# Expert matmuls with gate and up columns in one operand, down products one pair later, rows in blocks of 128

## The chip, the core and the metric

The kernel runs on one core of a Trainium2 chip. The core has TensorE (PE: matmuls, with weight loads PEld beside them), VectorE (DVE), ScalarE (ACT), GpSimd (POOL) and SyncE (SP), and 16 DMA engines that all queues share. The metric is the device time of one execution in microseconds, as the median of several runs. Profiles are taken from one execution, and all times in them count from the start of its span.

## The reference

The kernel computes four layers of cross attention and feed-forward on x of 4 x 256 rows of 256, each added to x after a layer norm. The change lies in the last step alone, a mixture of 64 experts of which every row chooses 8:

```python
x = hidden_states.reshape(-1, h)                       # 1024 rows of 256
router_logits = x @ gate_w                             # 64 logits
routing_weights, selected = jax.lax.top_k(router_logits, K)   # K = 8
routing_weights = jax.nn.softmax(routing_weights, axis=-1)
...
gate = jax.lax.ragged_dot(hidden_sorted, gate_proj_w, group_sizes)   # 256 -> 96
up = jax.lax.ragged_dot(hidden_sorted, up_proj_w, group_sizes)       # 256 -> 96
down = jax.lax.ragged_dot(jax.nn.silu(gate) * up, down_proj_w, group_sizes)  # 96 -> 256
...
out = jnp.sum(out * routing_weights[..., None], axis=1)
```

Everything is float32 in this step.

## The kernel before

All layers ahead of the experts run in one planned stretch (`layers`), with TensorE, VectorE, ScalarE, GpSimd and SyncE in a written order. At its end each tile of 128 rows is normed, routed, and scattered row by row to a table `hs` in device memory: expert e owns rows 192 e to 192 e + 191 (`CAP = 192`). A row of `hs` has 257 words, 256 of data and one with the number of its place in the results. There are 64 scatters of 128 rows, 8 choices for each of 8 tiles, issued by GpSimd (L1674). Rows that no token claims hold a number out of range, and are skipped when results are written. The tables `hs` and `yd` are filled early on by SyncE from constant tiles, `hs` in rows of 1,028 bytes and `yd` in rows of 1,024.

The experts are worked off in 32 pairs. `fill_rows` loads the 384 rows of a pair into a tile `hb` of 128 partitions x 3 rows: in the kernel before, partition q holds rows 3q, 3q+1 and 3q+2, one run of 3,084 bytes, and the first 64 partitions belong to the first expert. The loads of the first four pairs go to memory of earlier stages and are issued in `layers` by `first_rows` (the tiles `q`, `q`, `q`, `wmask` in the profile); each waits for the scatters of the choices that can reach its experts. Later ones run `AHEAD` = 6 pairs ahead in six buffers.

Weights come in groups of four experts (`load_weights`: 768 KB of gate and up, 384 KB of down, two DMAs), six groups in buffers `wt`. Groups 0 and 1 are loaded inside `layers` into memory that has become free (`cx` and `ctxT`). Weights and rows all go through SyncE's queue in the order of the code.

One pair, in the order of the code (`experts`):

- TensorE: gate sums `ps_g` and up sums `ps_u` (L1925), for each of two experts and two halves of the 256 inputs a matmul with 96 columns of weights against 192 rows, 8 in all
- ACT: `g` = silu(gate) (L1931); DVE: `act` = up x g (L1933), both over 96 x 384
- TensorE: the next pair's rows are transposed in 6 blocks of 128 x 128 (`rows_turned`, L1851), and copied to `hbT`, one half by ACT (L1936) and one by DVE (L1937)
- TensorE: down sums `ps_y` (L1943), for each of 3 rows of a partition and each expert a matmul with 64 columns of `act` against the 256 columns of `dn`, to the lower or upper 64 partitions
- DVE copies two of the three results to `yb` and ACT one (L1948); GpSimd puts them with three indirect DMAs (L1950) to `yd`, by the place numbers in `hb`
- beside that: in pairs 0 to 7 DVE works out the choice weights of one tile each (L1842 to L1844); in pairs 8 to 31 it makes diagonal matrices `diag` (L1965); loads of rows and weights are issued; from pair 23 on results are loaded back from `yd` (`load_results`, L1873) and some are added to x by DVE (L1885)

After the last pair `sums` adds the remaining results, half of the tiles by matmuls with `diag` (L1890), and stores x.

TensorE, DVE, ACT, POOL and SP execute in the order of the code here. f32 matmuls show as two records each in the profile, transposes as one. A branch with `rwo` handles rows that exceed an expert's 192 places; it is jumped over in this run.

Of the kernel before, what the change touches and what calls it, by code (L numbers as in the profile page):

```python
# [23 lines left out]
I32 = mybir.dt.int32  # L24
# [32 lines left out]
CAP = 192  # L57
RPP = 2 * CAP // P
# [172 lines left out]
def model(ctx: ExitStack, tc: tile.TileContext, a: dict, out: bass.AP):  # L231
# [155 lines left out]
    def expert_parts(gu, dn):  # L387
        return (
            gu.rearrange("p (e c i) -> p e c i", e=GROUP, c=4), dn.rearrange("p (e d) -> p e d", e=GROUP)
        )  # L390
# [35 lines left out]
    def fill_rows(p, since):  # L426

        ld = nc.sync.dma_start(
            hbs[p].rearrange("p j d -> p (j d)"),
            hs[2 * p * CAP : 2 * (p + 1) * CAP, :].rearrange("(p j) d -> p (j d)", p=P),  # L430
        )
        wanted = [i for n, js in zip(since, puts[: 2 * p + 2]) for i in js[n:]]
        needs(ld, "put", wanted, "rows of these choices alone")

    def layers(nk):
# [892 lines left out]
        def first_rows():  # L1328
            for p in range(in_early):
                yield Op(SP, 0.06, PUT[2 * p : 2 * p + 2], kb=386)  # L1330
                fill_rows(p, before)
# [422 lines left out]

    wts = [moe_tile([P, GROUP * (4 * I3 + D)], "wt", WEIGHTS)]
# [10 lines left out]
    def load_rows(p):  # L1766
        hbs[p] = moe_tile([P, RPP, HW], "hb", AHEAD)
        fill_rows(p, [0] * K3)
# [29 lines left out]
    with tc.If(rv > 0):  # L1798
# [9 lines left out]
        with tc.For_i(0, E3, 1) as e:  # L1808
# [4 lines left out]
            for c in range(NCH):  # L1813
                pg, pu = ps_mm([I3, CH], "ps_g3"), ps_mm([I3, CH], "ps_u3")
                for k, ps in enumerate((pg, pu)):
                    for dc in range(2):
                        o = (2 * k + dc) * I3
                        nc.tensor.matmul(
                            ps, gu[:, o : o + I3], hTs[c][:, dc, :], start=dc == 0, stop=dc == 1
                        )  # L1820
                g = moe_tile([I3, CH], "g_left", 1)
                nc.scalar.activation(g, pg, AF.Silu)
                nc.vector.tensor_mul(g, pu, g)
                for k in range(TPC):
                    t = c * TPC + k
                    y = ps_acc([P, D], "ps_y")
                    nc.tensor.matmul(y, g[:, k * P : (k + 1) * P], dn, start=True, stop=True)
                    w = scal(1, "w_left")
                    nc.vector.tensor_copy(w, rwo[:, t, bass.ds(e, 1)])
                    nc.vector.scalar_tensor_tensor(x_t(t), y, w, x_t(t), ALU.mult, ALU.add)  # L1830

    silu = small.tile([P, 1], F32, tag="silu", name="silu", bufs=1)
    diag = moe_tile([P, NT // 2, len(ON_PE), P], "diag", 1)
# [12 lines left out]
    def rows_turned(p):  # L1846
        hb, hbT = hbs[p], moe_tile([P, 2, RPP, P], "hbT", 2)
        tps = [ps_tp([P, RPP, P], "tp_hb") for _ in range(2)]
        for dc, tp in enumerate(tps):
            for j in range(RPP):  # L1850
                nc.tensor.transpose(tp[:, j, :], hb[:, j, dc * P : (dc + 1) * P], ident)  # L1851
        return hbT, tps
# [53 lines left out]

    def experts():
        for p in range(in_early, AHEAD):
            load_rows(p)
        load_weights(FIRST)  # L1910
        load_weights(FIRST + 1)
# [3 lines left out]
        hbT, tps = rows_turned(0)  # L1915
        nc.scalar.copy(hbT[:, 0], tps[0])
        nc.vector.tensor_copy(hbT[:, 1], tps[1])
        for p in range(n_pairs):
            e = 2 * p
            gu, dn = weights[e // GROUP]  # L1920
            pg, pu = ps_mm([I3, 2, RPP, P // 2], "ps_g3"), ps_mm([I3, 2, RPP, P // 2], "ps_u3")
            for k, ps in enumerate((pg, pu)):
                for i in range(2):
                    for dc in range(2):
                        nc.tensor.matmul(  # L1925
                            ps[:, i], gu[:, (e + i) % GROUP, 2 * k + dc, :],
                            hbT[:, dc, :, i * (P // 2) : (i + 1) * (P // 2)],
                            start=dc == 0, stop=dc == 1,
                        )
            g = moe_tile([I3, 2, RPP, P // 2], "g4", 2)  # L1930
            nc.scalar.activation(g, pg, AF.Silu)  # L1931
            act = moe_tile([I3, 2, RPP, P // 2], "act3", 2)
            nc.vector.tensor_mul(act, pu, g)  # L1933
            if p + 1 < n_pairs:
                hbT, tps = rows_turned(p + 1)
                nc.scalar.copy(hbT[:, 0], tps[0])  # L1936
                nc.vector.tensor_copy(hbT[:, 1], tps[1])  # L1937
            yb = moe_tile([P, RPP, D], "yb", 3)
            for js in ((0, 1), (2,)):
                y = ps_acc([P, len(js), D], "ps_y")  # L1940
                for k, j in enumerate(js):
                    for i in range(2):
                        nc.tensor.matmul(  # L1943
                            y[i * (P // 2) : (i + 1) * (P // 2), k], act[:, i, j, :],
                            dn[:, (e + i) % GROUP, :], start=True, stop=True,
                        )
                for k, j in enumerate(js):
                    (nc.scalar.copy if j == 1 else nc.vector.tensor_copy)(yb[:, j, :], y[:, k, :])  # L1948
            for j in range(RPP):
                put = nc.gpsimd.indirect_dma_start(  # L1950
                    out=yd[:, :],
                    out_offset=bass.IndirectOffsetOnAxis(
                        ap=hbs[p][:, j, D : D + 1].bitcast(I32), axis=0
                    ),
                    in_=yb[:, j, :], in_offset=None, bounds_check=NPAIR - 1, oob_is_err=False,
                )
                tc.declare_no_dep(put.ins, group="back", reason="distinct rows")
                tc.add_to_no_dep_group("back", put.ins)
                backs.append(put.ins)

            if p < NT:
                choice_weights(p)
            n, m = len(on_pe), n_pairs - NT
            for t, j in on_pe[max(p - NT, 0) * n // m : max(p - NT + 1, 0) * n // m]:
                nc.vector.tensor_scalar(  # L1965
                    diag[:, t // 2, j - ON_PE[0], :], ident, choice_w[:, t, j : j + 1], None, ALU.mult
                )
            if p + AHEAD < n_pairs:
                load_rows(p + AHEAD)
            k = FIRST + 2 + p if p < WEIGHTS - 2 else p // 2 + WEIGHTS if p % 2 else 0  # L1970
            if k and k < E3 // GROUP:
                load_weights(k)
            if p in loaded:
                load_results(loaded[p], p)
            for t, j in added_at.get(p, ()):
                add_result(t, j)
# [48 lines left out]

def laid_out(i):
# [38 lines left out]
        "w3_gu": gu.reshape(2, E3, 2, P, I3).transpose(3, 1, 0, 2, 4).reshape(P, E3, 4, I3),  # L2065
# [20 lines left out]
```

## Time and profile before

| what | value |
|---|---|
| median of 6 runs | 684.26 us (682.97 to 689.56) |
| the profiled execution | 686.94 us, span 685.2 us |
| start of pair 0's gate sums | 492.66 us |
| start of pair 1's gate sums | 500.36 us |
| start of pair 31's gate sums | 657.37 us |
| last put issued | 665.32 us |
| PE busy in the span | 612.9 us (89%) |
| POOL busy in the span | 401.9 us (59%), of it 96 puts of 0.97 us or a little more |

The profile's page gives for each engine the busy time in the span, and groups of instructions with the mean time of one. The stage table gives the same by stretches of time, with the granted clock of TensorE (1.00 is full) and the share of time that the 16 DMA engines were busy. The timeline lists instructions in order of time: start, length, engine, line, operation, output<-inputs, shapes, count of merged records, and in brackets how long the engine had been idle and what ended that.

From 500 to 600 us the pairs follow each other at 4.99 to 5.00 us, with one of 5.55 at 540. From 596.6 to 602 ACT and DVE were for the most part idle without a cause that the profile names, and the pairs that began at 595.83 and 604.94 took 9.11 and 6.64 us. Pair 30, beginning at 651.50, took 5.87. The end, from pair 31's gate sums to the end of the span, takes 27.8 us.

### The profile page before, as it was taken

What the parts mean: (1) busy time and instruction counts of PE and PEld (TensorE: products, weight loads), DVE (VectorE), ACT (ScalarE), POOL (GpSimd) and SP (SyncE); (2) the same over time, 40 slices, a digit from 0 to 9 for tenths busy, and PEclk for the clock granted to TensorE, in tenths of its full rate; (3) what the DMA queues carried; (4) which work ended last, traced back from release to release, by engine and by line L of the source; (5) the groups of instructions that cost most, each with busy time, mean ns of one, the idle gap of its engine ahead of it and who ended that gap; (6) DMA issues with size and microseconds to landing.
All of it is one profiled execution on the core that took longest, in us unless ns stands there. A gap on an engine that the chain in (4) does not pass through costs nothing. (4 is left out here: it accounts for less than half of the span.)

```text
span 685.2 us, 11415 instructions
## 1 busy us (share of the span) xinstructions
PE 612.9 (89%) x3831; PEld 469.3 (68%) x3844; DVE 444.7 (65%) x1094; ACT 349.7 (51%) x899; POOL 401.9 (59%) x531
## 2 busy tenths in 40 slices
PE   5998799989999999999999899397399999989965
PEld 4763367676787778778687678265377778868754
DVE  5688757876968795799786556344377544333655
ACT  2143248879788763667875875384322222222210
POOL 7997985045464536558268587717745655635650
PEclk9998899999999999999999999789599999989997
DMA  9999999611100230000031110202579988766567
GB/s 304 369 374 198 199 199 234 186 25 47 62 2 1 62 108 2 0 1 1 2 116 39 62 63 30 95 9 77 166 238 305 308 294 277 246 202 197 172 207 250
DMA packets 57059, 98.15 MB, mean 143 GB/s; under 512 B 7121, under 2 KB 39624, under 8 KB 56992
## 3 DMA queue, kind: packets, MB, share of 16 engines
q1 hardware_dynamic: 47072, 78.40, 40.2%
q0 software_dynamic: 7680, 16.84, 7.2%
q10 hardware_dynamic: 2240, 2.10, 1.0%
q8 instruction: 32, 0.52, 0.3%
q14 instruction: 35, 0.29, 0.1%
HBM read 58.42 MB, written 43.07 MB: 148 GB/s over the span
## 5 line engine op out<-in xcount | busy, mean ns | idle before, releaser
L1950 POOL DMA_INDIRECT yd<-yb,hb x84 | 83.2, 991 | 63.7 <-DVE yb L1948 44.4
L1674 POOL DMA_INDIRECT hs<-hx,slots x64 | 65.5, 1023 | 26.7 <-issue 13.7
L881 POOL TENSOR_TENSOR st<-st,mhalf 128x1 f32<-128x1 f32 x56 | 32.9, 591 | 56.5 <-DVE st L877 44.2
L1933 DVE TENSOR_TENSOR act<-ps_u,g 96x384 f32<-96x384 f32 x32 | 17.7, 554 | 49.6 <-ACT g L1931 24.7
L1505 POOL TENSOR_TENSOR q<-rt 64x512 f32<-64x512 f32 x32 | 42.5, 1328 | 10.9 <-DVE rt L1501 7.6
L1943 PE MATMUL ps_y<-wt,act 96*64 96x256 f32 x336 | 43.7, 397 | 5.7 <-DVE act L1933 4.5
L1538 ACT ACTIVATE e<-ps_s,nm 128x128 f32<-128x128 f32 x128 | 45.6, 393 | 5.6 <-DVE nm L1532 4.8
L1925 PE MATMUL ps_g<-hbT,wt 128*96 128x192 f32 x224 | 44.5, 343 | 0.0
L1948 DVE COPY yb<-ps_y 128x256 f32<-128x256 f32 x64 | 25.3, 422 | 28.2 <-PE ps_y L1943 25.4
L1925 PEld LDWEIGHTS ps_g<-hbT,wt 128*96 128x96 f32 x224 | 35.0, 167 | 11.4 <-issue 11.1
L1925 PE MATMUL ps_u<-hbT,wt 128*96 128x192 f32 x224 | 41.3, 328 | 0.0
L1948 ACT COPY yb<-ps_y 128x256 f32<-128x256 f32 x32 | 11.9, 372 | 54.9 <-DVE yb L1948 37.5
L1925 PEld LDWEIGHTS ps_u<-hbT,wt 128*96 128x96 f32 x224 | 36.8, 165 | 0.1
L1943 PEld LDWEIGHTS ps_y<-wt,act 96*64 96x64 f32 x336 | 22.1, 139 | 20.9 <-DVE act L1933 9.6
L1526 PEld LDWEIGHTS ps_s<-keys,q 128*128 128x128 f32 x256 | 35.4, 200 | 1.4
L1526 PE MATMUL ps_s<-keys,q 128*128 128x128 f32 x256 | 35.5, 284 | 0.0
L1576 PE MATMUL ps_u<-e,kvc 128*64 128x512 f32 x64 | 22.9, 633 | 13.5 <-ACT e L1562 11.3
L1931 ACT ACTIVATE g<-ps_g 96x384 f32<-96x384 f32 x32 | 15.6, 486 | 38.0 <-PE ps_g L1925 18.0
L1450 POOL TENSOR_TENSOR hh<-g,v 128x512 f32<-128x512 f32 x16 | 20.2, 1275 | 23.8 <-ACT g L1448 20.0
L1936 ACT COPY hbT<-tp_hb 128x384 f32<-128x384 f32 x31 | 14.8, 478 | 34.0 <-PE tp_hb L1851 16.0
L1532 DVE TENSOR_REDUCE nm<-ps_s 128x4 f32<-128x512 f32 x32 | 21.5, 684 | 16.4 <-remote 11.3
L1259 ACT ACTIVATE qT<-tp_q,rnd 128x512 bf16<-128x512 f32 (+2 forms) x48 | 25.7, 567 | 10.8 <-PE tp_q L1255 10.7
(344 smaller groups left out, 1726.2 us busy)
## 6 DMA issues: line engine op xcount, KB each, us to landing
hs<-order SPq DMA_DIRECT2D x1, 12336.0 KB
hb<-hs SPq DMA_DIRECT2D x28, 385.5 KB
wt<-in_w_gu SPq DMA_DIRECT2D x14, 768.0 KB
yd<-order SPq DMA_DIRECT2D x1, 8192.0 KB
wt<-yd SPq DMA_DIRECT2D x6, 1024.0 KB
wt<-in_w_dn SPq DMA_DIRECT2D x14, 384.0 KB
wo<-in_w_o SPq DMA_DIRECT2D x2, 1024.0 KB
w<-in_w SPq DMA_DIRECT2D x2, 704.0 KB
```

Of the source, the lines that this page charges most:

```text
L881: nc.gpsimd.tensor_tensor(s[:, 8:9], s[:, 7:8], mhalf, ALU.pow)
L1259: nc.scalar.activation(qT[:, 4 * i : 4 * i + full, :], tp.ap[:, :full, :], AF.Identity, bias=rnd[:, 1:2])
L1505: nc.gpsimd.tensor_add(qv(q[i])[r, hps, :], t0[r], t1[r])
L1526: nc.tensor.matmul(s.ap[:, k, :], qv(q[hd % 2])[:, hd // 2, rows], keys3[:, hd % 2, b * S : b * S + nk * P], start=False, stop=k == n - 1,)
L1532: nc.vector.tensor_reduce(nm[:, :n], s.ap, AX.X, ALU.max, negate=True)
L1538: nc.scalar.activation(wide[:, k, :], s.ap[:, k, :], AF.Exp, bias=nm[:, k : k + 1], accum_out=tot[:, k : k + 1],)
L1576: nc.tensor.matmul(o[r], kvc[:, 2 * b + kc, :], e[:, :, kc, :], start=kc == 0, stop=kc == nk - 1)
L1674: put = nc.gpsimd.indirect_dma_start(out=hs[:, :], out_offset=bass.IndirectOffsetOnAxis(ap=slots[:, t, j : j + 1], axis=0), in_=rows[:, j, ...
L1925: nc.tensor.matmul(ps[:, i], gu[:, (e + i) % GROUP, 2 * k + dc, :], hbT[:, dc, :, i * (P // 2) : (i + 1) * (P // 2)], start=dc == 0, stop= ...
L1943: nc.tensor.matmul(y[i * (P // 2) : (i + 1) * (P // 2), k], act[:, i, j, :], dn[:, (e + i) % GROUP, :], start=True, stop=True,)
L1948: (nc.scalar.copy if j == 1 else nc.vector.tensor_copy)(yb[:, j, :], y[:, k, :])
L1950: put = nc.gpsimd.indirect_dma_start(out=yd[:, :], out_offset=bass.IndirectOffsetOnAxis(ap=hbs[p][:, j, D : D + 1].bitcast(I32), axis=0), ...
```

## The change

What it does, part by part:

- The weights of an expert are laid out by the host as gate's 96 columns, then up's columns 64 to 95, then up's columns 0 to 63. The first 128 columns are one matmul operand (`ps_gu`, 128 x 384 for two experts); its partitions 0 to 95 are gate, 96 to 127 the upper part of up.
- Up's columns 0 to 63 are computed for the two experts of a pair side by side (`upper_sums`): expert 0 to partitions 0 to 63 of a tile, expert 1 to partitions 64 to 127, each against its own 192 rows.
- `act` is put together from three products: 32 rows over 384 columns, and twice 64 rows over 192 columns.
- Rows of a pair are loaded in three blocks of 128 (partition q holds rows q, 128 + q and 256 + q), so each piece of the load is one row of 1,028 bytes.
- Down: one matmul with 128 rows for each expert (`main_sums`), and the 64 remaining rows of each side by side (`rest_sums`). All three results are copied by ACT and put in the order 0, 2, 1.
- The down sums of pair p - 1 run in the turn of pair p, after its gate sums and the transposes for pair p + 1; then come `upper_sums` of p, then `rest_sums` of p - 1.
- The choice weights are worked out in every second one of the first 16 pairs, and the diagonals in the 16 after.
- Three groups of weights are issued before the rows of pair 3, which move from `first_rows` to `experts`. `diag` is allocated ahead of the weight buffers.

```diff
-            hbs[p].rearrange("p j d -> p (j d)"),
-            hs[2 * p * CAP : 2 * (p + 1) * CAP, :].rearrange("(p j) d -> p (j d)", p=P),
+            hbs[p], hs[2 * p * CAP : 2 * (p + 1) * CAP, :].rearrange("(j p) d -> p j d", p=P)
...
-            for p in range(in_early):
+            for p in range(in_early - 1):
...
+    lower, upper = slice(0, HALF), slice(HALF, P)
+    mine = (slice(0, CAP), slice(CAP, 2 * CAP))
+    whole = (slice(0, P), slice(HALF, CAP))
+    rest = (slice(P, CAP), slice(0, HALF))
+
+    def upper_sums(hbT, gu, g, act):
+        ps = ps_mm([P, CAP], "ps_u3")
+        for dc in range(2):
+            for i, c in enumerate((lower, upper)):
+                nc.tensor.matmul(
+                    ps[c], gu[:, i, dc, P:], hbT[:, dc, mine[i]], start=dc == 0, stop=dc == 1
+                )
+        for i, c in enumerate((lower, upper)):
+            nc.vector.tensor_mul(act[:HALF, i], ps[c], g[:HALF, i])
+
+    def main_sums(act, dn):
+        y = ps_acc([P, 2, D], "ps_y")
+        for i in range(2):
+            nc.tensor.matmul(y[:, i], act[:, i, whole[i]], dn[:, i], start=True, stop=True)
+        return y
+
+    def rest_sums(act, dn):
+        y = ps_acc([P, D], "ps_r")
+        for i, c in enumerate((lower, upper)):
+            nc.tensor.matmul(y[c], act[:, i, rest[i]], dn[:, i], start=True, stop=True)
+        return y
...
+    def beside(p):
+        if p < 2 * NT and p % 2 == 0:
+            choice_weights(p // 2)
...
+        k = FIRST + 3 + p if p < WEIGHTS - 3 else p // 2 + WEIGHTS if p % 2 and p > 3 else 0
...
     def experts():
-        for p in range(in_early, AHEAD):
+        for k in range(3):
+            load_weights(FIRST + k)
+        for p in range(in_early - 1, AHEAD):
             load_rows(p)
-        load_weights(FIRST)
-        load_weights(FIRST + 1)
...
+        for p in range(n_pairs + 1):
+            if p < n_pairs:
...
+                ps = ps_mm([P, 2, CAP], "ps_gu")
+                for i in range(2):
                     for dc in range(2):
                         nc.tensor.matmul(
+                            ps[:, i], gu[:, i, dc, :P], hbT[:, dc, mine[i]], start=dc == 0, stop=dc == 1
                         )
+                g = moe_tile([I3, 2, CAP], "g4", 2)
+                nc.scalar.activation(g, ps[:I3], AF.Silu)
+                own = hbT
+                act = moe_tile([I3, 2, CAP], "act3", 2)
+                if p == 0:
+                    upper_sums(own, gu, g, act)
+                if p + 1 < n_pairs:
+                    hbT = rows_turned(p + 1)
+                nc.vector.tensor_mul(act[HALF:], ps[I3:], g[HALF:])
+            if p > 0:
+                yb = moe_tile([P, RPP, D], "yb", 3)
+                y = main_sums(*before)
+                for i in range(2):
+                    nc.scalar.copy(yb[:, 2 * i, :], y[:, i])
+                if p < n_pairs:
+                    upper_sums(own, gu, g, act)
+            if p > 0:
+                nc.scalar.copy(yb[:, 1, :], rest_sums(*before))
+                put_results(p - 1, yb)
+                beside(p - 1)
+            if p < n_pairs:
+                before = act, dn
...
+def inner_columns(gu):
+
+    gate, up = gu
+    return np.concatenate([gate, up[..., HALF:], up[..., :HALF]], axis=-1)
...
-        "w3_gu": gu.reshape(2, E3, 2, P, I3).transpose(3, 1, 0, 2, 4).reshape(P, E3, 4, I3),
+        "w3_gu": inner_columns(gu).reshape(E3, 2, P, 2 * I3).transpose(2, 0, 1, 3),
```

## The prediction

> **What bounds the kernel now.** I read the stage table first, to find where a pair of experts is paid for, then the timeline of one pair, then the start of the loop, then the DMA view. Only the part after 487 us is touched by the change. The stage table (start:end, length, then busy us and instruction count of PE, PEld, DVE, ACT, POOL, then granted clock, DMA share, GB/s):
>
> ```profile
> 493.00:500.00 7.00, 5.76 (x32) 4.62 (x33) 1.34 (x3) 1.76 (x3) 2.47 (x5) 0.81 0.55 180
> 500.00:540.00 40.00, 39.51 (x274) 32.07 (x272) 31.37 (x56) 10.69 (x24) 23.78 (x24) 1.00 0.99 295
> 560.00:600.00 40.00, 38.99 (x270) 31.69 (x266) 15.43 (x38) 9.63 (x22) 23.21 (x24) 1.00 0.79 259
> 600.00:610.00 10.00, 7.82 (x34) 5.78 (x34) 2.34 (x5) 1.97 (x5) 3.06 (x4) 0.66 0.78 251
> ```
>
> TensorE is busy all the time. DMA is full as well up to 560 us, at 0.79 after that. The disturbance at 600 is told below. One pair in the timeline (start, length):
>
> ```profile
> 560.90 1.22 PEld L1925 LDWEIGHTS ps_g<-hbT,wt 128*96 128x96 f32 x8 [0.39 <-issue]
> 561.50 0.97 POOL L1950 DMA_INDIRECT yd<-yb,hb  x1 [1.52 <-DVE yb L1948]
> 562.12 1.30 PEld L1925 LDWEIGHTS ps_u<-hbT,wt 128*96 128x96 f32 x8
> 562.78 0.97 POOL L1950 DMA_INDIRECT yd<-yb,hb  x1 [0.30 <-issue]
> 563.42 0.74 PEld L1851 LDWEIGHTS tp_hb<-ident,hb 128*128 128x128 f32 x6
> 563.84 0.55 DVE L1933 TENSOR_TENSOR act<-ps_u,g 96x384 f32<-96x384 f32 x1 [2.08 <-issue]
> 564.44 1.06 PEld L1943 LDWEIGHTS ps_y<-wt,act 96*64 96x64 f32 x12 [0.28 <-issue]
> 565.89 0.24 PEld L1925 LDWEIGHTS ps_g<-hbT,wt 128*96 128x96 f32 x2 [0.39 <-issue]
> ```
>
> The reader is to see the period: 565.89 - 560.90 = 4.99 us. Every f32 matmul shows as two records. Gate and up are 16 records from 560.90 to 563.42, 2.52 us or 0.157 each; the 6 transposes take 0.74; then TensorE stands 0.28 for DVE's product `act` (563.84 + 0.55); the 12 down records take 564.44 to 565.89, 1.45 us or 0.121 each. A down record streams 256 columns and a gate record 192, yet the down record is shorter: the two 64-column halves run side by side. POOL's puts are spaced 1.28 us (562.78 - 561.50), so three are 3.84 a pair.
>
> The start, and what a pause does:
>
> ```profile
> 487.38 5.92 SPq L428 DMA_DIRECT2D q<-hs  x3
> 492.66 2.96 PE L1925 MATMUL ps_g<-hbT,cx 128*96 128x192 f32 x8
> 500.30 0.32 SPq L428 DMA_DIRECT2D wmask<-hs  x1
> 502.52 0.37 SPq L1762 DMA_DIRECT2D wt<-in_w_gu  x1
> 507.88 0.74 PEld L1851 LDWEIGHTS tp_hb<-ident,wmask 128*128 128x128 f32 x6
> 602.18 2.83 PE L1943 MATMUL ps_y<-wt,act 96*64 96x256 f32 x12 [2.85 <-DVE act L1933]
> ```
>
> Rows of pairs 0 to 2 are loaded as soon as their scatters have landed (487.4 to 493.3), those of pair 3 at 500.30, and only then the first weights. At 602 TensorE had waited 2.85 us because ACT and DVE stood; the same 12 records then took 2.83 in place of 1.52, at a granted clock of 0.66.
>
> **The change, part by part.**
>
> *Gate and up.* 16 records of 0.157 become 8 with 128 columns and the same 192 streamed, 8 x 0.157 = 1.26. The wider weight load does not set the pace: the 128-column loads of `ps_sum` go at 1.70 / 8 = 0.2125 for 256 streamed columns, the same rate per column as 0.157 for 192. The other 8 records are the 64-column ones of two experts side by side, which the trace of before has only in the down product. Scaled by columns they cost 8 x 0.121 x 192/256 = 0.73; if they do not overlap, 8 x 0.157 = 1.26. I take 0.73, since the form is that of the down rows.
>
> *Down.* 12 records become 4 of full width, 4 x 0.2125 = 0.85, and 4 side by side, 4 x 0.121 = 0.48: 1.33 against 1.45.
>
> *Order.* Down of pair p-1 now runs in pair p's turn, after the transposes. Its operand `act` was finished in the turn before, so the wait of 0.28 goes. In place of it the next possible wait is TensorE for `hbT` of the next pair, ready a copy (0.56) after the transposes, with 2.06 us of down and up sums in front: no wait.
>
> Sum for TensorE: 1.26 + 0.74 + 0.85 + 0.73 + 0.48 = 4.06 us a pair against 4.99.
>
> *The other engines at 4.06.* ACT: silu 0.49, copy 0.48, three results 3 x 0.37, 2.08 in all. DVE: copy 0.56, 32-row product 0.55, two products of 192 columns. A line through its rows 256 -> 0.42 and 512 -> 0.69 gives 0.35 each, so 1.81. The choice weights (three operations of 0.69, L1842 to L1844, 2.1 us) move from each of 8 pairs to every second of 16, so two pairs need 5.7 of 8.1. Both have room, and if DVE were late its `hbT` copy would be what stalls. POOL at 3.84 has 0.22 left. The put of a pair waits for ACT copies alone, and `yb` has three buffers, 12 us, while a put lands within 3.
>
> *Row loads in blocks of 128.* Each load is now 384 pieces of 1,028 bytes in place of 128 of 3,084. The DMA view of two windows holds the two nearest prices, the fill of `yd` (1,024-byte rows, 30 to 50 us) and of `hs` (1,028-byte rows, 50 to 70 us):
>
> ```profile
> DMA packets 7548, 7.72 MB, mean 386 GB/s; under 512 B 14, under 2 KB 7548, under 8 KB 7548
> DMA packets 3924, 4.05 MB, mean 202 GB/s; under 512 B 2, under 2 KB 3923, under 8 KB 3923
> ```
>
> So a 1,028-byte piece costs between 42 and 82 ns of one of 16 engines, a load 1.0 to 2.0 us, against about 1.0 now (394,752 bytes at 390 GB/s). Both rows are writes to memory; results 2 are read back in 1,024-byte pieces at 374 to 391 GB/s (650 to 653 us), and the 3,084-byte row loads, unaligned too, reach 432 GB/s near 490. The change makes reads, so I take 1.1 and keep 2.0. DMA need per pair now: 0.79 x 4.99 = 3.95, so 4.05 after, level with TensorE. Row loads run 6 pairs (24 us) ahead and weights 10, which covers small lateness.
>
> The Trainium skill, "DMA: Bandwidth & Descriptors", Specifications, says that 512 bytes and more move at line rate. By it the split costs nothing and the total would be the same 662, the lead hiding the difference. The 202 GB/s row contradicts it for writes of 1,028 bytes.
>
> *Early weights.* Three groups (six DMAs, 3.54 MB) are issued on SP right after pair 2's rows, near 493.5, ahead of the rows of pair 3, which still wait for the last scatters until about 500.3. From 493.5 to 500.3 the DMA was 0.55 busy, so about half of 6.8 us x 390 GB/s, 1.0 to 1.8 MB, goes through. What is left, 1.7 to 2.5 MB (4.5 to 6.5 us), stands before pair 3's rows if the queue serves in order: with 1 us of transfer and 1.5 of latency they land at 507.3 to 509.3, say 508.3. They would be wanted at 504: gu(1) starts near 499 (pair 0 without its down sums), one turn, 1.26. So TensorE waits some 4 us, and by the row at 602 runs slow after it; I charge 2.0 (that pause cost about 1.3 on the down sums, 1.3 on the gate sums and 0.4 on the up sums, and fewer sums follow here). Gate of pair 3 then starts at 508.3 + 0.74 + 0.85 + 0.73 + 0.48 + 2.0 = 513.1, against 510.36 before: 2.7 lost. Bounds: 5 better if the rows are in time, 4 worse if the weights themselves wait for the scatters.
>
> The Trainium skill, "TensorE: Matmul & The Clock Gate", the section on why this matters for kernels, warns against idle gaps over about 3 us between bursts, which speaks against this part. The 2.85 us gap at 602 was followed by slow records, so the trace agrees. Without that charge the forecast would be 660.
>
> *Pairs 3 to 31.* 28 turns at 0.93 less: 26.0 gained. The disturbances there (4.1 and 1.6 us at 600 to 611, 0.9 at 655, 0.5 at 544) I leave as they are. Adding of results 0 and 1 moves with its pair: its load went out at 627.41 and was used at 637.14; 3 turns of 4.06 are 12.2 us, enough for 8.5.
>
> *The end.* The last pair has no transposes and its down sums wait for two products of 0.35. Its last put is issued about as long after its gate sums as now (7.95 us). But the last put of pair 30 comes 1 us later relative to them, and with it the load of results 4 and 5, which the end waits for (663.59 + 8.21): 1.0 lost.
>
> Sum: -26.0 + 2.7 + 1.0 = -22.3. The profiled execution took 686.94 us (span 685.2); it becomes 664.6. The median of 684.26 lies 2.7 below it, so I predict 684.3 - 22.3 = 662.
>
> **The rivals.**
>
> *The halves of 64 do not overlap.* Then a turn is 4.06 + 0.53 = 4.59: 28 x 0.53 = 15 more, 677. For it: no row has 128 input rows with 64 columns. Against: the 12 down records at 0.121.
>
> *Row pieces at the price of the `hs` fill.* A pair needs 3.95 - 1.0 + 2.0 = 4.95 of DMA while weights come, pairs 3 to 20. Lateness of 17 x 0.89 = 15 less the 7 us of lead left after the start is 8: 670. For it: the 202 GB/s row. Against: those are writes.
>
> *POOL takes over (slower).* The puts are spaced 1.28 and one in the loop took 1.68 while DVE added results (page mean 991 ns). In the new loop DVE works more densely beside them. From a spacing of 4.99 / 3 = 1.66 on, nothing is gained; at 1.68 + 0.30 = 1.98 a turn is 5.94, and 31 turns cost 29 more than now: 713. Against: from 500 to 540 DVE was busy 78% and the puts stayed at 0.97 to 1.05.
>
> *The change does not do what it says:* weights that wait for the scatters after all. That is the worse bound of the early weights, 666, within the forecast.
>
> **How the numbers follow.** Forecast 0.64 (its own range 655 to 670: 652 with the start in time and the pause at 600 gone; 666 with weights late, 3 more for a turn of 4.16), rows at the fill's price 0.10, halves apart 0.13, POOL or another engine at 4.9 or more a turn 0.13. The last I split into slower 0.10 and same 0.03; the rest, 0.87, is faster. The range 650 to 680 takes in the first three. Half a percent, 3.4 us, is about what this kernel's runs can tell from no change.
>
> **What would show it.** Right: turns of 4.0 to 4.2 us; the 8 half records in 0.7 to 0.8 us; pair 3's transposes waiting for the `wmask` load until about 508, with slow records after; puts still 0.97. Wrong: half records at 0.157; idle time of POOL near zero with TensorE waiting for ACT copies, and these for DMA; row loads of 2 us and `tp_hb` waiting for `hb` past pair 8.

## The result, and the profile after

The changed kernel took 692.0 us (median of 20 runs, 688.98 to 699.07) against 685.61 for the kernel before on the same chips (46 runs, 679.69 to 689.66). The ratio on record is 1.0105, with a 95% interval of 1.0084 to 1.0126 (it is not the quotient of the two medians, which is 1.0093): slower by one per cent, where 662 was forecast. The profiled execution took 695.59 us (span 693.8), 31 us more than the 664.6 that the prediction's sum gives for a profiled execution. By stretches of the two profiles:

| stretch, us | before | forecast | after | after less forecast |
|---|---|---|---|---|
| first transposes of rows start at | 491.2 | 491.2 | 493.2 | +2.0 |
| from there to the gate sums of pair 3 | 19.1 | 21.9 | 27.2 | +5.3 |
| gate of pair 3 to gate of pair 31, 28 turns | 147.0 | 121.0 | 137.6 | +16.6 |
| of it 28 undisturbed turns | 28 x 4.99 | 28 x 4.06 | 28 x 4.254 | +5.4 |
| of it pauses (what is left) | 7.3 | 7.3 | 18.5 | +11.2 |
| gate of pair 31 to the end of the span | 27.8 | 28.8 | 35.8 | +7.0 |

The 2.0 us at the first row lie ahead of the early weights: the rows of pair 0 already leave at 489.20 for 487.38. They are not explained; that start lies between 486.4 and 493.2 us in the profiles of most versions.

The table of stretches after, with the columns shown of before (start:end, length, busy us and count of PE, PEld, DVE, ACT, POOL, granted clock, DMA share, GB/s):

```profile
493.00:500.00 7.00, 5.97 (x28) 4.55 (x28) 1.08 (x3) 2.35 (x4) 4.20 (x7) 0.69 0.79 253
500.00:540.00 40.00, 30.48 (x189) 23.56 (x190) 18.65 (x37) 11.52 (x31) 16.20 (x16) 0.87 0.90 271
560.00:600.00 40.00, 39.19 (x268) 30.71 (x266) 22.09 (x45) 16.20 (x44) 24.48 (x25) 0.97 0.83 265
600.00:610.00 10.00, 5.70 (x36) 4.73 (x35) 2.69 (x8) 2.17 (x6) 5.78 (x7) 0.83 0.75 232
```

From 500 to 540 TensorE was busy 39.5 us before and is busy 30.5 now; most of that is the start. From 600 to 610 it has 5.7 of 10, and that is a pause.

One undisturbed turn of the changed kernel, by the weight loads in its timeline (start, length, engine, line, what):

```profile
542.77 1.27 PEld L1985 LDWEIGHTS ps_gu<-hbT,wt 128*128 128x128 f32 x8 [0.39 <-issue]
544.02 0.74 PEld L1852 LDWEIGHTS tp_hb<-ident,hb 128*128 128x128 f32 x6
544.73 0.73 PEld L1928 LDWEIGHTS ps_y<-wt,act 96*128 96x128 f32 x4
545.79 0.52 PEld L1919 LDWEIGHTS ps_u<-hbT,wt 128*64 128x64 f32 x8 [0.33 <-issue]
546.34 0.31 PEld L1934 LDWEIGHTS ps_r<-wt,act 96*64 96x64 f32 x4
547.03 0.30 PEld L1985 LDWEIGHTS ps_gu<-hbT,wt 128*128 128x128 f32 x2 [0.39 <-issue]
```

The period is 547.03 - 542.77 = 4.26 us (4.25 in most turns). From start to start: gate and up 1.25, transposes 0.71, whole down sums 1.06, up halves 0.55, down halves 0.69. The eight half records lie in 0.55 us, so the two experts' halves do run side by side. What is longer than forecast are two steps from one group to the next, 0.33 and 0.39 us of "issue", in which the engine waited for nothing that the profile shows. The step of 0.39 ahead of the gate sums stood in the old turn too (at 560.90 and 565.89); the one of 0.33 is new.

The start after, in the timeline:

```profile
496.82 0.01 SPq L1763 DMA_DIRECT2D wt<-in_w_gu  x1
500.94 0.44 SPq L1763 DMA_DIRECT2D wt<-in_w_dn  x1
504.04 0.39 SPq L429 DMA_DIRECT2D wmask<-hs  x1
514.94 1.51 PE L1852 MATMUL tp_hb<-ident,wmask 128*128 128x128 f32 x6 [8.16 <-DMA wmask<-hs]
518.09 1.55 PE L1919 MATMUL ps_u<-hbT,ctxT 128*64 128x192 f32 x8
```

The first early weight load leaves SyncE's queue at 496.82 and the last at 500.94; pair 3's rows follow at 504.04 (before: 500.30) and are there at 514.94 (before: by 507.88, without a wait for them). TensorE stands 8.16 us and then runs slowly, 1.55 us for up sums that take 0.87 in an undisturbed turn.

A pause, in the timeline:

```profile
601.43 0.82 PE L1852 MATMUL tp_hb<-ident,hb 128*128 128x128 f32 x6
...
602.93 0.97 POOL L1939 DMA_INDIRECT yd<-yb,hb  x1 [0.30 <-issue]
...
603.75 0.60 PE L1934 MATMUL ps_r<-wt,act 96*64 96x256 f32 x4
604.21 0.97 POOL L1939 DMA_INDIRECT yd<-yb,hb  x1 [0.30 <-issue]
605.48 0.97 POOL L1939 DMA_INDIRECT yd<-yb,hb  x1 [0.30 <-issue]
605.95 0.49 ACT L1989 ACTIVATE g<-ps_gu 96x384 f32<-96x384 f32 x1 [3.29 <-issue]
...
608.12 0.56 DVE L1854 COPY hbT<-tp_hb 128x384 f32<-128x384 f32 x1 [6.35 <-remote]
608.12 0.48 ACT L1853 COPY hbT<-tp_hb 128x384 f32<-128x384 f32 x1 [1.69 <-remote]
...
608.66 2.61 PE L1985 MATMUL ps_gu<-hbT,wt 128*128 128x192 f32 x7 [4.30 <-ACT hbT L1853]
```

TensorE's transposes are over at 602.3 and its whole turn at 604.4. VectorE has stood for 6.35 us before it copies those transposes, and ScalarE copies the other half in the same moment, 608.12. GpSimd issues put after put all the while. Then the gate sums are slow, 2.61 us, at a granted clock of 0.50:

```profile
608.00:610.00 2.00, 1.34 (x4) 1.34 (x5) 1.78 (x5) 1.31 (x4) 0.85 (x1) 0.50 1.05 402
```

The trace also has the times at which semaphores were raised, the counters by which engines wait for each other. TensorE raises one semaphore for all its sums and transposes. Around this pause its raises are on record at 602.27 and then six times from 608.05 to 608.34, though the work that the six stand for ended between 601.9 and 604.4 by the profile. VectorE's copy starts 0.07 us after the first of the six. So ScalarE and VectorE do not stand by themselves: what releases them comes late. The pause in the kernel before looks the same: raises for sums and transposes that ended from 597.37 to 599.33 are on record only from 601.49 to 601.59.

The end, in the timeline:

```profile
654.27 1.66 DVE L1888 SCALAR_TENSOR_TENSOR x<-wt,choice_w,x 128x256 f32<-128x256 f32 x4
654.31 2.47 POOL L1939 DMA_INDIRECT yd<-yb,hb  x1 [0.30 <-issue]
...
664.19 1.73 PE L1928 MATMUL ps_y<-wt,act 96*128 96x256 f32 x4 [2.54 <-DVE act L1923]
...
672.68 0.97 POOL L1939 DMA_INDIRECT yd<-yb,hb  x1 [0.30 <-issue]
677.29 2.07 PE L1893 MATMUL ps_sum<-wt,diag 128*128 128x256 f32 x4 [5.42 <-DMA wt<-yd]
```

A put that starts beside VectorE's four additions takes 2.47 us; three more took 2.09 to 2.67 from 650 on. The last put goes out 14.7 us after the gate of pair 31 (657.98), where it was 7.95 before, and from it to the end it takes 21.1 us (before 19.9).

### The profile page after: what moved, and what is told of

It is laid out like the page before. It is cut to its first block, busy times and chain, and to the rows that moved or that the text cites. A ratio compares the mean times of both kernels' runs of the same rounds, so it can differ in the third digit from the quotient of the medians.

```text
span 693.8 us, 11154 instructions
## 1 busy us (share of the span) xinstructions
PE 601.8 (87%) x3703; PEld 457.2 (66%) x3716; DVE 444.6 (64%) x1094; ACT 366.4 (53%) x963; POOL 410.0 (59%) x531
## 5 line engine op out<-in xcount | busy, mean ns | idle before, releaser
L1674 POOL DMA_INDIRECT hs<-hx,slots x64 | 65.7, 1027 | 27.9 <-issue 13.7
L1985 PE MATMUL ps_gu<-hbT,wt 128*128 128x192 f32 x224 | 48.0, 360 | 10.4 <-ACT hbT L1853 10.2
L1854 DVE COPY hbT<-tp_hb 128x384 f32<-128x384 f32 x32 | 17.8, 558 | 56.2 <-PE tp_hb L1852 18.0
L1985 PEld LDWEIGHTS ps_gu<-hbT,wt 128*128 128x128 f32 x224 | 38.6, 202 | 22.0 <-ACT hbT L1853 12.9
L1923 DVE TENSOR_TENSOR act<-ps_u,g 64x192 f32<-64x192 f32 x64 | 22.7, 355 | 26.4 <-PE tp_hb L1852 7.5
L1989 ACT ACTIVATE g<-ps_gu 96x384 f32<-96x384 f32 x32 | 15.6, 488 | 43.5 <-PE ps_gu L1985 13.0
L2001 ACT COPY yb<-ps_y 128x256 f32<-128x256 f32 x64 | 20.7, 377 | 27.9 <-PE ps_y L1928 19.1
L1928 PE MATMUL ps_y<-wt,act 96*128 96x256 f32 x112 | 30.2, 393 | 2.9 <-DVE act L1923 2.5
L1259 ACT ACTIVATE qT<-tp_q,rnd 128x512 bf16<-128x512 f32 (+2 forms) x48 | 25.7, 567 | 11.1 <-PE tp_q L1255 11.0
L1562 ACT COPY e<-tp_e 128x512 f32<-128x512 f32 x32 | 18.4, 613 | 23.1 <-remote 11.2
L1491 PE MATMUL ps_q<-qc,wq 96*128 96x256 f32 x128 | 30.4, 380 | 0.0
L884 DVE TENSOR_SCALAR h<-x,st 128x256 f32<-128x256 f32 x56 | 26.7, 488 | 5.6 <-POOL st L881 5.3
L1163 ACT ACTIVATE e<-ps_s,nb 128x256 f32<-128x256 f32 x64 | 30.1, 493 | 0.0
```

The lines of the kernel that those rows point to most:

```text
L884: nc.vector.tensor_scalar(h[:, k, :], x_t(t), ss[k][:, 6:7], ss[k][:, 8:9], ALU.subtract, ALU.mult)
L1163: nc.scalar.activation(e[:, mt, :], s[:, mt, :], AF.Exp, bias=nb[:, mt : mt + 1], accum_out=tot[:, 2 * j + mt : 2 * j + mt + 1],)
L1259: nc.scalar.activation(qT[:, 4 * i : 4 * i + full, :], tp.ap[:, :full, :], AF.Identity, bias=rnd[:, 1:2])
L1491: nc.tensor.matmul(ps.ap[:, k, :], w[:, hp * P : (hp + 1) * P], qc.ap, start=True, stop=True)
L1674: put = nc.gpsimd.indirect_dma_start(out=hs[:, :], out_offset=bass.IndirectOffsetOnAxis(ap=slots[:, t, j : j + 1], axis=0), in_=rows[:, j, ...
L1928: nc.tensor.matmul(y[:, i], act[:, i, whole[i]], dn[:, i], start=True, stop=True)
```

## The experiments

All are measured against the kernel before on the same chip. "Start" is the time from the first transposes to the gate of pair 3, "pauses" the time from there to the gate of pair 31 beyond 28 undisturbed turns (of 4.254 us, or 4.99 for the old loop), "end" the time from that gate to the span's end; these three come from one profile each.

| kernel | median us | ratio [95%] | start | pauses | end |
|---|---|---|---|---|---|
| kernel before | 684.26 | 1 | 19.1 | 7.3 | 27.8 |
| changed kernel | 692.0 | 1.0105 [1.0084, 1.0126] | 27.2 | 18.5 | 35.8 |
| rows_first | 680.86 | 0.9946 [0.9914, 0.9977] | 16.4 | 13.5 | 37.9 |
| before_early | 693.8 | 1.0139 [1.0071, 1.0208] | 26.6 | 4.1 | 28.1 |
| row3_first | 690.3 | 1.0062 [1.0024, 1.0101] | 16.3, then 11 lost at pair 4 | 14 | 36.6 |
| contig | 691.14 | 1.0113 [1.0047, 1.0179] | 25.7 | 15.8 | 36.9 |
| no_adds | 691.54 | 1.0081 [1.0052, 1.0109] | 27.9 | 17.5 | 33.1 |
| no_weights | 693.49 | 1.0102 [1.0040, 1.0164] | 28.4 | 15.1 | 37.1 |
| no_rows | 695.31 | 1.0123 [1.0073, 1.0173] | 28.1 | 18.2 | 37.6 |
| yb5 | 691.79 | 1.0090 [1.0058, 1.0122] | 26.9 | 13.4 | 37.0 |
| one_put | 668.03 | 0.9743 [0.9715, 0.9772] | 29.2 | 0.0 | 26.9 |
| no_data_again | 686.03 | 1.0101 [1.0072, 1.0130] | 28.1 | 12.1 | 35.1 |
| after_again | 688.14 | 1.0154 [1.0104, 1.0205] | 26.7 | 12.7 | 36.9 |

The last two shared a chip on which the kernel before took 678.4 us.

**The start: rows first again.**

```diff
-            for p in range(in_early - 1):
+            for p in range(in_early):
                 yield Op(SP, 0.06, PUT[2 * p : 2 * p + 2], kb=386)
...
-        for k in range(3):
-            load_weights(FIRST + k)
-        for p in range(in_early - 1, AHEAD):
+        for p in range(in_early, AHEAD):
             load_rows(p)
+        load_weights(FIRST)
+        load_weights(FIRST + 1)
...
-        k = FIRST + 3 + p if p < WEIGHTS - 3 else p // 2 + WEIGHTS if p % 2 and p > 3 else 0
+        k = FIRST + 2 + p if p < WEIGHTS - 2 else p // 2 + WEIGHTS if p % 2 else 0
```

> The changed kernel with the order of loads as it was before: the rows of pairs 0 to 5 first, then the weights (pair 3's rows are asked for ahead of the five weight loads). Theory (early weights delay pair 3's rows: its gate ran at 520.4 us against 510.4 before, and 1.9 of these 10.1 us were there ahead of the scatters): the gate of pair 3 comes 7 to 9 us earlier against the scatters' end, the time falls by 6 to 9 us to 683 to 686 us. Rival (the loop is held by its pauses and by the puts, so what is won at its start is lost behind): the gate comes earlier, but the time stays within 2 us of 692. Second rival (the weights missing later hold pair 4 or 6): the gate of pair 3 is early and another gate of pairs 4 to 8 waits 3 us or more for wt.

The timeline of this kernel at the same place:

```profile
501.41 0.36 SPq L429 DMA_DIRECT2D wmask<-hs  x1
...
503.71 0.48 SPq L1763 DMA_DIRECT2D wt<-in_w_gu  x1
...
509.23 1.57 PE L1985 MATMUL ps_gu<-hbT,ctxT 128*128 128x192 f32 x8
514.24 1.57 PE L1985 MATMUL ps_gu<-hbT,wt 128*128 128x192 f32 x8 [0.68 <-ACT hbT L1853]
```

The first weight load leaves at 503.71, 7 us later than in the changed kernel, and yet the gate sums of pair 4, the first that need it, start at 514.24 and wait for no weights. The time is 11 us lower, more than the 6 to 9 expected, and the kernel is half a per cent faster than the kernel before. So the early weights were needed by nobody in time, and they held up the rows. The other way round, the same order of loads in the kernel before (`diag` is also allocated earlier there, as in the changed kernel):

> The kernel before with nothing changed but the order of loads: five weight loads ahead of the rows of pairs 3 to 5, as in the changed kernel. Theory (the early weights cost what putting the rows first won, whatever the matmuls are): the gate of pair 3 comes 8 us later against the first transposes than before, the time rises by 6 to 11 us (ratio 1.009 to 1.016). Rival (the early weights hurt the changed kernel alone, whose turns are short): ratio 0.997 to 1.004.

8.6 us slower (693.8 against 685.23), of it 7.5 in the start, where TensorE now waits for pair 3's rows:

```profile
514.72 1.51 PE L1852 MATMUL tp_hb<-ident,wmask 128*128 128x128 f32 x6 [5.78 <-DMA wmask<-hs]
```

The price belongs to the order of the loads, whatever matmuls follow. Last, pair 3's rows alone ahead of the weights (`in_early` in both places, the weight order of the changed kernel kept):

> The changed kernel with the rows of pair 3 asked for ahead of the five weight loads, the rows of pairs 4 and 5 still behind them. Theory (it is pair 3's rows alone that are late, and by the queue they stand in): the gate of pair 3 as with all rows first, 16 to 17 us after the first transposes instead of 27, time 680 to 684. Rival (the weights beside the scatters fill the DMA engines, so every row load behind the scatters is late, in whatever place): a gate of pair 3 or 4 waits for rows 4 us or more, time 686 to 691.

The time and the late pair are the rival's, but its reason fails: pair 3's rows, ahead of the weights, are as early as with all rows first, so it is not every load behind the scatters that is late. The rows of pair 4, behind the weights, are late by as much as pair 3's were. The timeline:

```profile
518.49 1.51 PE L1852 MATMUL tp_hb<-ident,hb 128*128 128x128 f32 x6 [8.23 <-DMA hb<-hs]
```

In these runs, whichever rows stand behind the 3.5 MB of weights come late.

**The row pieces.** The old rearrangement of the load, in the changed kernel:

```diff
-            hbs[p], hs[2 * p * CAP : 2 * (p + 1) * CAP, :].rearrange("(j p) d -> p j d", p=P)
+            hbs[p].rearrange("p j d -> p (j d)"),
+            hs[2 * p * CAP : 2 * (p + 1) * CAP, :].rearrange("(p j) d -> p (j d)", p=P)
```

> The changed kernel with each pair's rows loaded as before, three rows of 1,028 bytes running on in a partition (each row then goes through another expert of its pair than its own; as much is moved and computed). Theory (the pieces of 1,028 bytes cost nothing that decides): time within 2 us of 692, the loop's pauses between the gates of pairs 3 and 31 still 15 to 20 us in sum. Rival (pieces of 1,028 bytes fill the DMA engines and so make the pauses of ScalarE and VectorE): the pauses fall to about 7 us as before, the loop is 8 to 11 us shorter, the time 680 to 685.

Time and pauses stay. Pieces of 1,028 bytes cost nothing that decides here.

**The end: no additions beside the puts.**

```diff
-        for t, j in added_at.get(p, ()):
-            add_result(t, j)
```

> The changed kernel without the 24 additions of the results of choices 0, 1 and 2 (they are left out of the output). Theory (VectorE's additions of two SBUF operands hold up GpSimd's puts, five of which took 1.9 to 2.7 us instead of 0.97, and the puts run late behind the last pair): the puts of pairs 26 to 31 take 0.97 to 1.1 us, from the gate of pair 31 to the end it takes 28 to 30 us instead of 35.8, and the time falls by 6 to 8 us to 684 to 686. Rival (the puts are late because the turns are short, 3.84 us of puts against 4.25 a turn, and the end hangs on the load of the last results): the end stays over 33 us and the time falls by less than 3 us.

The puts from pair 26 on all take 0.97 to 0.98 us, as foreseen, so the additions are what stretched them. But, as the rival had it, the end falls only from 35.8 to 33.1 and the time stays where it was: the last put still goes out 12.2 us after the gate of pair 31. The Trainium skill, "SBUF — State Buffer", section on who interferes with whom, says that a VectorE instruction with two SBUF inputs contends with a GpSimd instruction that reads SBUF, through a port pair that is an exclusive lock. The rows that bear on it, a put of 2.47 us beside 1.66 us of additions against 0.97 without them, agree with it. The five puts of 1.36 to 1.66 us that are left in this run lie beside the choice weights (L1843, L1844), which take both inputs from SBUF too.

**The pauses: what they do not come of.** Three runs take one suspect each out of the changed kernel. no_weights returns from `load_weights` for groups 8 to 15 with the weights of groups 6 and 7; no_rows loads only column `D` of the rows from pair 6 on; yb5 writes `"yb", 5`. A fourth goes the other way, rows turned two pairs ahead on top of rows_first (three buffers `hbT`).

> The changed kernel without the weight loads of groups 8 to 15 (experts 32 to 63 are computed with the weights of groups 6 and 7); the loop then moves 9.2 MB less. Theory (the pauses, in which ScalarE and VectorE stand together for 2 to 6 us while TensorE has work done, come of full DMA engines): the pauses between the gates of pairs 5 and 31 fall from 18 us to under 6, the loop is 10 us or more shorter, the time 678 to 683. Rival (the pauses come of the three result buffers that wait for their puts, or of something in the engines' own instruction streams): the pauses stay at 14 us or more and the time at 688 or more.

> The changed kernel in which pairs 6 to 31 load only the row numbers of their rows (4 bytes of 1,028 each) and turn the rows of pairs 0 to 3 again; weights and puts stay. Theory (the pauses of ScalarE and VectorE begin where SyncE sends two pairs' rows off together, so they come of the row loads): pauses between the gates of pairs 3 and 31 under 6 us instead of 18.6, time 676 to 682. Rival (they come of the puts, or of nothing that is loaded): pauses 12 us or more, time 686 to 692.

> The changed kernel with five buffers for a pair's results instead of three, so that ScalarE's copies wait for puts two pairs older. Theory (the loop's pauses do not come of that wait: VectorE, which waits for no put, stands as long as ScalarE): pauses between the gates of pairs 3 and 31 within 4 us of 18.6, time 689 to 694. Rival (they come of copies that wait for a put that has not landed): pauses under 10 us, time 680 to 685.

> The kernel with all rows first, and each pair's rows turned two turns ahead (three buffers instead of two), so that a pair's gate never waits for the copies made in the turn just before. Theory (the pauses cost what goes beyond the 2.5 us of TensorE work between the transposes and the next gate; with the gate as further cover, 1.25 us more of each is hidden): pauses between the gates of pairs 3 and 31 fall from 13.6 us to 6 to 10, time 674 to 679. Rival (whatever holds ScalarE and VectorE holds TensorE at the next transposes or down sums just as well): pauses 12 to 15 us, time 679 to 683.

None takes the pauses away: 15.1, 18.2 and 13.4 us of them remain, and the times stay at 691.8 to 695.3. In the case of no_weights and no_rows that was against the theory. yb5 lies between its theory (14.6 or more) and its rival (under 10), much nearer the theory. rows_first_ahead2 was 695.24 us (1.0149 [1.0083, 1.0215]), slower than rows_first by 14 and outside both of its expectations: its transposes now waited for rows in ten turns behind pair 3, 1.4 to 3.3 us each. So rows that are wanted one turn sooner are not there. Eight buffers for rows (`"hb", AHEAD + 2`, also on top of rows_first) do not help either:

> The kernel with all rows first, and eight buffers for rows instead of six, each still asked for six pairs ahead: a row load then waits for a put two pairs older. Theory (SyncE stands at a row load until a put lands and then sends two pairs' rows and weights off at once, which makes the pauses): row loads go out one at a time about 4.5 us apart, pauses fall from 13.6 us to under 8, time 673 to 677. Rival (the pauses do not hang on when rows are asked for): pauses 11 to 16 us, time 678 to 683.

681.4 us (0.9941 [0.9904, 0.9979]): the rival by the time, with pauses of 18.5, more than it expected.

**The pauses: what they do come of.**

```diff
-        for j in (0, 2, 1):
+        for j in (0,):
             put = nc.gpsimd.indirect_dma_start(
```

> The changed kernel with one of the three puts of each pair (two thirds of the results are left out). Theory (the pauses come of the row loads, not of the puts; the end, though, is 8 us longer because the puts run late): pauses between the gates of pairs 3 and 31 stay at 12 us or more, from the gate of pair 31 to the end 27 to 30 us instead of 35.8, time 680 to 686. Rival (GpSimd's puts make the pauses too): pauses under 6 us, time 668 to 676.

668.03 us, 24 less than with three puts, on a chip with the kernel before at 685.5. All 28 turns take 4.25 us, up to 4.29; there is no pause at all. The four timed runs lie within 1.5 us of each other, where those of the changed kernel spread over 10. The waits of VectorE from 524 to 640 us (what waited, for what: us in total, times, longest), the longest entry of this kernel and after it the longest of no_data_again below:

```profile
DVE hbT L1854 <- PE tp_hb L1852: 28.9, 17, 1.8
```

```profile
DVE hbT L1854 <- PE ps_r L1934: 16.1, 6, 3.7
```

With one put VectorE is released by the transposes that it copies; in all 28 turns its copy starts at most 0.28 us after their end. With three it is released late, when TensorE is two or three groups further, up to 3.09 us after the end of the transposes in no_data_again and 5.87 in the changed kernel. The theory on record, that puts do not make the pauses, fell here, and its rival was right in kind. The end is 26.9 us, just under the 27 to 30 that the theory had for it.

Is it what the puts write? The changed kernel with `bounds_check=127`, so that nearly every row is dropped:

> The changed kernel with all three puts, of which only rows with a place under 128 are written (nearly all results are left out), once more. On a chip with pauses (kernel before at 683 to 687 us). Theory (the pauses come of GpSimd's issue at its limit): 10 us or more of pauses between the gates of pairs 3 and 31, time 684 to 692. Rival (they come of the writing of the puts' rows): under 4 us, time 670 to 678. On a chip without pauses (before at about 663): 657 to 661 as before, which tells nothing of them.

12.1 us of pauses against 12.7 in the changed kernel on the same chip, and DMA traffic from 524 to 640 us at 191 GB/s against 236. So the pauses come with three issued puts a turn and not with the rows that are written. What of a put makes them stays open. Besides GpSimd's issuing, each put raises semaphores when it lands, written rows or not: on the chip of the next runs 1,999 such raises of DMAs are on record in the loop with three puts and 1,236 with one. And where there are pauses, records are missing: of 196 raises by TensorE between the gates of pairs 3 and 31, 167 are on record in the changed kernel and 166 in no_data_again, but 195 in one_put. Whether the raises, or their recording for the profile, take part in the pauses is a rival that no run here tests. The changed kernel beside no_data_again:

> The changed kernel, unchanged. On a chip with pauses: 690 to 694 us and 13 to 20 us of pauses. On a chip without them (before at about 663): the loop from the gate of pair 3 to that of pair 31 takes 119 to 122 us, the start still loses 8 us to the early weights and the end some 7 us to the puts, so the time is 656 to 661, ratio 0.990 to 0.998.

688.14 us and pauses of 12.7, a little under both figures, on a chip where the kernel before takes 678.4.

**Runs that could not decide.** Three runs fell on a chip where the kernel before takes 662.83 us and where no loop shows a pause:

> The changed kernel with two of the three puts of each pair (a third of the results is left out). Theory (the pauses come where GpSimd has no idle time to catch up: three puts take 3.84 us of a turn of 4.25, two take 2.56): no pause over 1 us between the gates of pairs 3 and 31, time 669 to 673. Rival (each put has its chance of a pause): pauses about two thirds of those with three, 9 to 13 us, time 680 to 684.

> The changed kernel with all three puts, of which only rows with a place under 128 are written and all others are dropped (nearly all results are left out): GpSimd issues as much, and the DMA engines write next to nothing for it. Theory (it is GpSimd's issue that is at its limit): pauses between the gates of pairs 3 and 31 of 10 us or more, puts still 1.28 us apart, time 684 to 692. Rival (it is the writing of the puts' rows that makes the pauses): pauses under 4 us, time 672 to 680.

> The changed kernel with one put of each pair and two memsets of 128x1024 on GpSimd in place of the other two (two thirds of the results are left out): GpSimd is as busy, with a third of the puts. Theory (GpSimd's full time alone makes the pauses): 10 us or more, time 680 or more. Rival (puts make them, as DMA work, not GpSimd's time): pauses under 3 us, time 667 to 672.

They took 654.47, 658.86 and 650.83 us, with pauses of 0.1, 0.3 and 0.0 us. No_data has all three puts and no pauses there (and all of TensorE's 196 raises are on record), so nothing of this tells what makes them elsewhere, and whether GpSimd's time or the puts as such matter stays open. Their ends agree with the rest: 30.4, 35.7 and 27.1 us with two, three and one put a pair.

**A version faster than both.** In rows_first a new wait stood at the end:

```profile
651.09 2.05 PE L1928 MATMUL ps_y<-wt,act 96*128 96x256 f32 x4 [5.57 <-DVE act L1923]
```

VectorE stood for a result of choice 2 that had not landed, in front of pair 31's product. Its eight additions were moved behind the last pair, alone and then with five `yb` buffers:

> The kernel with all rows first, and the eight additions of choice 2 behind the last pair instead of beside pairs 29 and 30. Theory (with rows first, pair 31's sums waited 5.6 us at 651 us for VectorE, which stood at an addition whose result had not landed): that wait falls under 1.5 us, the end from 37.9 to 32 to 34 us, time 675 to 678. Rival (the end hangs on the load of the last results, which waits for the last put alone): the wait is gone but the end falls by less than 2 us, time 679 to 681.

> The kernel with all rows first, five result buffers and the additions of choice 2 behind the last pair. Theory (each buffer more lets ScalarE run on when puts are late; the last addition no longer holds pair 31): time 674 to 679, below both kernels by 1 to 1.5 per cent. Rival (GpSimd's puts set the pace, so buffers only move the wait): 680 to 682 as with rows first alone.

The wait went, but alone the time stayed at 681.46 (0.9931 [0.9899, 0.9963]): TensorE then waited 6.7 us for results to be read back. That is the rival, nearly. With five buffers, on the chip without pauses, 654.38 against 662.83: 0.9869 [0.9852, 0.9885]. The changed kernel was not measured on that chip. The loop of that version is not free of waits either: it takes 9.2 us more than 28 undisturbed turns, most of it TensorE waiting for rows, which this view from 494 to 618 us sums up:

```profile
PE tp_hb L1852 <- DMA hb<-hs: 8.0, 6, 1.7
```

On chips with pauses rows_first, rows_first_hb8 and rows_first_adds_last are alike the fastest complete versions, 3 to 4 us under the kernel before and some 11 under the changed one.

## Why the prediction was wrong

- **The turn** was mis-sized by 0.19: forecast 4.06, measured 4.25. The halves came out at 0.55 where 0.73 was charged, the whole down sums at 1.06 for 0.85 and the down halves at 0.69 for 0.48, because of the two steps of 0.33 and 0.39 us between groups. The step of 0.39 was in the prediction's own row: its 0.121 a down record is 1.45 us for twelve, of which their loads take 1.06, so a step that does not shrink with the records was shared out among them. The other step, 0.33, the prediction did not have. Of 26.0 us, 20.6 were really gained here. The rival of halves that do not overlap is refuted.
- **Early weights** is the step that failed by most in one place. It set 1.0 to 1.8 MB of the 3.54 MB to go through before 500 us, because the DMA engines were idle by half. But the weights left the queue only from 496.82 on, not near 493.5, and in those 7 us the engines moved 253 GB/s for 180, which is 0.5 MB more. About 3 MB stood in front of pair 3's rows in place of 1.7 to 2.5, and the rows themselves were sent 3.7 us later than before. They landed at 514.9 for a forecast of 508.3. The prediction priced 2.7 us for it; rows_first shows 11 us in the time and before_early 8.6. The bound of 4 us on the bad side, set for weights that wait for the scatters, was exceeded by 1.3. That TensorE would run slowly after such a wait was right.
- **"The disturbances there I leave as they are"** is the second step that failed, by 11.2 us. The prediction had listed them, the largest at 600, and took them over unchanged without asking what they were. They come with three puts a turn and not with one (one_put), and in the short turn the same puts came, in these profiles, with two and a half times as much pause, 18.5 us for 7.3. Why the puts bring them stays open.
- **The end** was forecast 1.0 longer, as the last put was to follow the gate of pair 31 at the same distance. It went out 14.7 us after it for 7.95. Three puts take 3.84 us of each 4.25, so GpSimd catches up at most 0.41 us of a delay in a turn, and with down sums one turn later the puts of two pairs stand at the end in a row. That this makes up the 12.2 that remain with puts at 0.97 (no_adds) is argued, not shown, though the end falls to 26.9 with one put a pair. The other 2.5 are puts that VectorE's additions held up.
- **POOL takes over** was the rival on the slower side, with 0.10. Its sign was right and GpSimd was the place. Its mechanism was not: the puts in the loop stayed 1.28 us apart and the undisturbed turn 4.25. GpSimd set the pace through pauses and through the end.
- **Row pieces at the price of the `hs` fill** is refuted by contig. That rows would still be there in time was right for the loop as built, though rows_first_ahead2 shows that less than one turn was to spare.
- "Puts still 0.97" held for the median. None of the rivals had the start, the pauses and the end all wrong at once.

## What to carry to other kernels

A load that is moved forward in a shared queue pays only if somebody waits for it; price it by who stands behind it, and read from the trace when the queue would really issue it. Before an engine's work is made denser, look at the engine that does not become shorter: at 3.84 us of 4.25 GpSimd had little left to make up a late put, and most of the time came back in pauses and in the end. A disturbance in the profile is a term of the sum like any other, and the shorter loop need not leave it as it was.

## What the runs showed of the hardware

- ScalarE and VectorE can stand together for 2 to 6 us while what they wait for on TensorE is long done by the profile, and start in the same moment (608.12 above), within 0.1 us of TensorE's semaphore raises, which are on record late and bunched (six from 608.05 to 608.34). On the chips that show it, it came with three GpSimd puts a turn, also with hardly a row written (12.1 us), and not with one (0.0). How the puts delay the raises is not shown.
- It hangs on the chip. On one of the chips the kernel before took 662.8 us in place of 678 to 686, its runs lay within 2.2 us, and no version showed a pause of this kind. Most of the difference lies ahead of the experts: the first transposes of rows start at 472.9 to 475.3 us in the versions profiled there, against 486.4 to 493.2 elsewhere. A ratio from one chip need not hold on another: three puts a pair without written rows were 0.9933 there and 1.0101 on a chip with pauses.
- Pauses cost twice: after 4.30 us without work the next gate sums took 2.61 us instead of 1.57, at a granted clock of 0.50 between 608 and 610.
